# A GNN layer on one core: results handled in block order, n gate's half copied out of PSUM by ScalarE, start-up loads and planner costs rearranged

## The chip, the core and the metric

The kernel runs on 1 core of one Trainium2 chip. The metric is the device time of one execution, in microseconds (us). Three executions of the kernel before took 1700.17, 1704.7 and 1708.09 us, median 1704.7. Engines: PE is TensorE (matrix multiplication), DVE VectorE, ACT ScalarE, POOL GpSimd, SP SyncE, which only issues DMAs here.

## The reference, cut to what matters

64 graphs of 256 nodes with 256 features. All is float32.

```
h = maximum(layernorm(x), 0)                      # x: (64, 256, 256)
xc = transpose(h)
c = relu(bn1(conv1d(xc, conv1_w)))                # width 1
c = bn2(conv1d(c, conv2_w, pad 8))                # width 17, along the nodes
x_conv = transpose(relu(c + xc))
s = h @ w_se.T + b_se                             # 3 values a node
A = exp(-squared distance of s) * adj
x_nmp = A @ relu(h @ w_msg.T + b_msg)
gi = concat(x_conv, x_nmp) @ w_ih.T + b_ih        # 512 -> 768
gh = h @ w_hh.T + b_hh                            # 256 -> 768
r, z = sigmoid(gi_r + gh_r), sigmoid(gi_z + gh_z)
n = tanh(gi_n + r * gh_n)
out = x + (1 - z) * n + z * h
```

## The kernel before, in words

**Tiles and stages.** Graphs are worked in pairs (W = 512 columns: two graphs of 256 nodes, channels on partitions) and pairs in blocks of four (8 graphs); there are NP = 32 pairs and NB = 8 blocks. The 17-tap convolution is done by short Fourier-like transforms along the nodes: `forward` (DVE) makes the tiles U, V, PT and Sv of a block, PE multiplies them with 47 transformed filters (`begin`, `complete`, `product`, L930-L965), and `join` (DVE) transforms back. The filters are made once, in the start-up: `filter_steps` (L1278) multiplies the raw weights (`taps`) with `points`, ACT copies the results out of PSUM, and SP and POOL store them in turn in DRAM (`filt`). From there each block loads them again, one filter of 256 KB a time, into nine slots `wb` (`load_kinds`, L905).

**A block.** First come the products with the filters; between them stand pieces of other pairs' work (`message`, `embed`, `affinity`, `aggregate`). Then `gates(i)` to `gates(i+3)` compute the GRU gates of the four pairs. `gates` calls `seven` (L1155) twice, once for r and z, once for n; each takes two PSUM accumulators `acc0` and `acc1` (a ring of two, L573) and four `aux` banks (L572), and its matmuls run in the order of parts 1, 5, 2, 6, 7, 3, 4. Six of the nine slots hold sums of activations for these parts, one (`e`) a copy, two (`tz0`, `tz1`) tanh of z. Part 7 is the last reader of the sums `ah`, `axn`, `axc`; after `gates(i+3)` they are given back (L1475) and `load_kinds` (L1477) starts the filter loads of the next block. The boundary between blocks is thus: part 7, 3 and 4 of the last n gate, the rest of the next pair's `message`, then `begin(0)` of the next block, whose product needs a filter slot, Sv and a free accumulator.

**The n gate** (L1190-L1204). For each half `dc` of the channels ACT reads `gh_n` out of the accumulator's second half; DVE multiplies it with r; DVE then reads the first half of the accumulator (`halfs(p, 0)`, L1195) and adds. Until that last read the accumulator is not free. tanh (ACT), three DVE operations and two ACT copies into `back` follow; the copies take the 16-bit halves of the result apart.

**Results.** `finish` (L1245) transposes `back` by a DMA into `gn_tile`. `deliver` (L1260) puts the halves together again (two ACT copies), adds x to each graph by an accumulating DMA on POOL's queue (L1268), and writes each graph to DRAM by another (L1269). Both address DRAM through `rows` (L588): partition h*16 + b holds two node rows at b*16 + 2h, so the DRAM side is 8 x 16 runs of 2 KB. `blocks` (L609) has partition b*8 + h instead, and its DRAM side is 128 runs one behind the other.

**The order of the work** isn't the order of the calls. `Recorder.record` (L334) notes every operation with a cost by engine and shape, and `plan` (L388) then puts them into each engine's queue: PE's calls get due times from the running sum of PE's costs, all others a due time back from what needs them, and at each step the engine that can start first takes its most urgent call. DMA costs (L342-L351) and ACT costs (L362-L367) enter there. All instructions are emitted from one place and therefore have the line L371 in the profile; groups are told apart by the tiles' names. Calls between `nc.first = 0` (L704) and L721 keep their order ahead of all others.

**Start-up loads** (L704-L721), on SP's queue: x of four pairs, then for each half `dc` the first three groups of taps (112 partitions, `load_taps`) and the remaining 7 partitions of all 18 groups at once (`load_last_taps`), then points 1 to 3, then the further groups. A group's matmul needs both pieces. While the four pairs are normalized and go through the first convolution, `filter_steps((1, 2, 3, 3)[j])` (L1298) hands out nine of the 55 filter steps between them.

Of the kernel before, what the change touches and what calls it, by code (L numbers as in the profile page):

```python
# [14 lines left out]
U16 = mybir.dt.uint16  # L15
# [234 lines left out]
class Recorder:  # L250
# [83 lines left out]
    def record(self, engine, op, args, kw):  # L334
        method = getattr(getattr(self.nc, engine), op)
        out = kw["out"] if "out" in kw else args[0]
        ins = [v for v in list(args) + list(kw.values()) if isinstance(v, bass.AP) and v is not out]
        n = 1
        for s in out.shape[1:]:
            n *= s  # L340
        size = 0
        if op.startswith("dma"):  # L342
            if "transpose" in op:
                size, cost = 2.5, self.TURN
            elif "accum_op" in kw:
                size, cost = 2.3, 1.0
            else:
                k = max(self.share(out, ins[0]), 10 if engine == "gpsimd" else 1)
                run = min(self.run(v) for v in (out, ins[0]))
                size = n * out.shape[0] * WIDTH[out.dtype] * 16 / k / 330e3 * max(1, 1400 / run)  # L350
                cost = 0.35 if k > 10 and run > 1024 else 0.62  # L351
        elif engine == "tensor":
            cost = n / 597 + 0.006
            if op == "transpose":
                cost = out.shape[-1] / 1170
            elif args[1].shape[0] < 32:
                cost = 0.23
        elif engine == "vector":
            cost = {"bn_stats": 0.33, "bn_aggr": 0.07}.get(op, n / 960 + 0.07)
            if op == "tensor_mul" and n == 256:  # L360
                cost = 0.5
        elif engine == "scalar":  # L362
            cost = n / 1400 + (0.2 if op == "activation" else 0.12)
            if out.dtype == U16:
                cost = n / 860
            elif len(out.shape) == 3 and op == "activation" and n == 256:
                cost = 0.49  # L367
        else:
            cost = 1.1 if self.planned == 0 else 7.0 if ALU.pow in args else 2.0
        k = len(self.tasks)  # L370
        self.tasks.append(Task(engine, lambda: method(*args, **kw), cost, size, self.first))  # L371
        self.last[engine] = k
        if self.behind is not None:
            self.tasks[k].preds.add(self.behind)
        if self.first is not None:
            self.first += 1
        for v in ins:
            self.access(k, v, False)
        self.access(k, out, True)
        return k  # L380
# [106 lines left out]
def kernel(  # L487
# [124 lines left out]
    def load_x(i, eng=nc.sync):  # L612
        if i >= NP:
            return
        X[i] = SPARE[i].rearrange("p (q d) -> p q d", d=D) if i in SPARE else x_rows
        load_rows(X[i], x, i, eng, blocks if i <= PB else rows)
# [56 lines left out]

    def load_taps(dc, a, b, eng):
        v = c2_wT[dc * P + a * KG:dc * P + b * KG].rearrange("(g k) t o -> (k t) g o", k=KG)
        eng.dma_start(out=taps[:MAIN, a:b, dc, :], in_=v[:MAIN])

    def load_last_taps(dc, eng):
        v = c2_wT[dc * P:dc * P + FULL * KG].rearrange("(g k) t o -> (k t) g o", k=KG)
        eng.dma_start(out=taps[MAIN:KG * TAPS, :FULL, dc, :], in_=v[MAIN:])  # L680

    def load_last_group(dc, eng):
        last = c2_wT[dc * P + FULL * KG:(dc + 1) * P]
# [24 lines left out]
    load_points(0, nc.scalar)  # L708
    for j in range(PB):
        load_x(j)  # L710
    for dc in range(DC):
        load_taps(dc, *PARTS[0], nc.sync)
        load_last_taps(dc, nc.sync)
    for n in range(1, len(PASSES) + 1):
        load_points(n, nc.sync)
    for part in PARTS[1:]:
        for dc in range(DC):
            load_taps(dc, *part, nc.sync)
# [456 lines left out]
    def halfs(p, k):  # L1175
        return p[:, :, k * N:(k + 1) * N]

    def pieces(t):
        return t.rearrange("p (g n) -> p g n", n=N)

    def gates(i, between=None):
        tr, gn = tr_tile, gn_tile
        tz = [slots[ROLE[f"tz{dc}"]].rearrange("p c d -> p (c d)") for dc in range(DC)]

        def rz(dc, p):
            for gate, t in ((0, tr[:, dc]), (1, tz[dc])):
                nc.scalar.activation(pieces(t), halfs(p, gate), AF.Tanh,
                                     bias=b_rz[:, gate * DC + dc:gate * DC + dc + 1], scale=0.5 - dc)

        def n(dc, p):  # L1190
            g = gn[:, dc]
            nc.scalar.activation(pieces(g), halfs(p, 1), AF.Identity,
                                 bias=b_hh[:, 2 * DC + dc:2 * DC + dc + 1], scale=1.0 - 2 * dc)
            nc.vector.scalar_tensor_tensor(g, tr[:, dc], 1.0, g, op0=ALU.add, op1=ALU.mult)
            nc.vector.scalar_tensor_tensor(pieces(g), pieces(g), 0.5, halfs(p, 0), op0=ALU.mult,  # L1195
                                           op1=ALU.subtract if dc else ALU.add)
            nc.scalar.activation(g, g, AF.Tanh, bias=b_ih[:, 2 * DC + dc:2 * DC + dc + 1])
            d = tr[:, dc]
            nc.vector.tensor_sub(d, HT[i][:, dc], g)
            nc.vector.scalar_tensor_tensor(d, tz[dc], 1.0, d, op0=ALU.add, op1=ALU.mult)  # L1200
            nc.vector.scalar_tensor_tensor(d, d, 0.5, g, op0=ALU.mult, op1=ALU.add)
            u = d.bitcast(U16).rearrange("p (n j) -> p j n", j=2)
            for j in range(2):
                nc.scalar.copy(back.bitcast(U16).rearrange("p (c j n) -> p c j n", c=DC, j=2)[:, dc, j], u[:, j])  # L1204

        def last(dc, g, p):
            a = slice(g * N, (g + 1) * N)
            v, d = gn[:, dc, a], tr[:, dc, a]
            nc.scalar.activation(v, p[:, N:], AF.Identity,
                                 bias=b_hh[:, 2 * DC + dc:2 * DC + dc + 1], scale=1.0 - 2 * dc)  # L1210
            nc.vector.scalar_tensor_tensor(v, d, 1.0, v, op0=ALU.add, op1=ALU.mult)
            nc.vector.scalar_tensor_tensor(v, v, 0.5, p[:, :N], op0=ALU.mult, op1=ALU.subtract if dc else ALU.add)
            nc.scalar.activation(v, v, AF.Tanh, bias=b_ih[:, 2 * DC + dc:2 * DC + dc + 1])
            nc.vector.tensor_sub(d, HT[i][:, dc, a], v)
            nc.vector.scalar_tensor_tensor(d, tz[dc][:, a], 1.0, d, op0=ALU.add, op1=ALU.mult)
            for c in range(MC):
                t = chunk(y_last[:, dc], g, c).rearrange("p (b h) -> p h b", b=NW)
                u, w = (q[:, c * P:(c + 1) * P].rearrange("p (h b) -> p h b", b=NW) for q in (d, v))
                nc.vector.scalar_tensor_tensor(t, u, 0.5, w, op0=ALU.mult, op1=ALU.add)

        seven(i, RZ, rz)
        if between:
            between()
        if i + 1 < NP:
            seven(i, NH, n)
            return
        a0, p5, e1, a1, e0 = aux(), aux(), aux(), acc()[:, 1], acc()[:, 0]
        e = slots[ROLE["e"]].rearrange("p c d -> p (c d)")
        part(a0, 1, i, NH, True)
        nc.scalar.mul(e0, a0, -1.0)  # L1230
        part(p5, 5, i, NH, True)
        nc.scalar.copy(e, p5)
        part(a0, 2, i, NH)
        last(0, 0, a0)
        part(e0, 6, i, NH)
        nc.vector.tensor_add(a1, e0, e)
        part(e0, 7, i, NH)
        nc.vector.scalar_tensor_tensor(e1, e0, -1.0, e, op0=ALU.mult, op1=ALU.subtract)
        last(1, 1, e1)
        part(a1, 3, i, NH)  # L1240
        last(0, 1, a1)
        part(e0, 4, i, NH)
        last(1, 0, e0)
# [16 lines left out]
    def deliver(i):  # L1260
        y = back.rearrange("p (q d) -> p q d", d=D)
        t = gn_tile.rearrange("p c n -> p (c n)").bitcast(U16)
        v = y.bitcast(U16).rearrange("p q (c d j) -> p j c q d", c=DC, j=2)
        u = t.rearrange("p (c j q d) -> p j c q d", j=2, c=DC, d=P)
        for j in range(2):
            nc.scalar.copy(v[:, j], u[:, j])
        for g in range(G):
            nc.gpsimd.dma_start(out=row_tile(y, g), in_=rows(x, G * i + g), accum_op=ALU.add)  # L1268
            nc.gpsimd.dma_start(out=rows(out, G * i + g), in_=row_tile(y, g))  # L1269

    FIRST = PARTS[1][1]
    steps = deque((m, g) for g in range(FIRST) for m in range(len(PASSES)))
# [19 lines left out]
    for j in range(PB):  # L1292
        if j > 0:
            norm(j)
        transpose_h(j)
        conv1(j, True)
        split(j)
        filter_steps((1, 2, 3, 3)[j])  # L1298
    *bn2, b_ih, b_hh = columns("bn2")
    s2, h2_shift = fold_bn(bn2, "bn2", 1.0 / L)  # L1300
    b_rz = keep("b_rz", 2 * DC)
# [222 lines left out]
```

## Time and profile before

| | |
|---|---|
| three executions, us | 1700.17, 1704.7, 1708.09 |
| the profiled execution, us | 1703.87 |
| its span, first to last instruction, us | 1702.1 |
| TensorE clock granted, mean | 0.994 |
| DMA bytes moved | 261.47 MB, mean 154 GB/s |

| engine | busy, us | what runs on it |
|---|---|---|
| PE | 1666.3 | 8984 matmuls; a float32 matmul of the code is two of them |
| DVE | 1457.8 | transforms, gates, layernorm |
| ACT | 1052.4 | copies out of PSUM, exp, tanh, copies of 16-bit halves |
| POOL | 231.8 | 62 accumulating loads and 62 stores of results among its DMA issues |

An engine's busy time says how long its instructions ran; a group of instructions is shown with its count, busy time and mean, and with the idle time of the engine just ahead of it. The timeline has start, duration and, in brackets, the idle time ahead and what ended it. A block takes about 200 us: from 300 to 400 us lies mostly the products' part of one, from 400 to 500 us mostly the gates' part.

### The profile page before, as it was taken

What the parts mean: (1) busy time and instruction counts of PE and PEld (TensorE: products, weight loads), DVE (VectorE), ACT (ScalarE), POOL (GpSimd) and SP (SyncE); (2) the same over time, 40 slices, a digit from 0 to 9 for tenths busy, and PEclk for the clock granted to TensorE, in tenths of its full rate; (3) what the DMA queues carried; (4) which work ended last, traced back from release to release, by engine and by line L of the source; (5) the groups of instructions that cost most, each with busy time, mean ns of one, the idle gap of its engine ahead of it and who ended that gap; (6) DMA issues with size and microseconds to landing.
All of it is one profiled execution on the core that took longest, in us unless ns stands there. A gap on an engine that the chain in (4) does not pass through costs nothing.

```text
span 1702.1 us, 26181 instructions
## 1 busy us (share of the span) xinstructions
PE 1666.3 (98%) x8984; PEld 1420.8 (83%) x8984; DVE 1457.8 (86%) x3401; ACT 1052.4 (62%) x1967; POOL 231.8 (14%) x245
## 2 busy tenths in 40 slices
PE   8999999999999999999999999999999999999998
PEld 5888878988889788888888887897888978898886
DVE  7969989799889998799997998979987899879545
ACT  5546665685657765676655866567575766556453
POOL 4211130022110121102110021101211012100010
PEclk9999999999999999999999999999999999999999
DMA  9982666966579366773559554694756836484032
GB/s 228 306 280 69 137 117 142 280 136 140 108 196 241 94 127 124 218 208 89 122 113 293 136 116 110 160 273 97 144 112 191 233 91 125 88 245 129 17 60 52
DMA packets 326812, 261.47 MB, mean 154 GB/s; under 512 B 204751, under 2 KB 252139, under 8 KB 326678
## 3 DMA queue, kind: packets, MB, share of 16 engines
q1 hardware_dynamic: 296982, 216.71, 48.4%
q0 software_dynamic: 29280, 42.76, 13.1%
q8 instruction: 71, 1.16, 0.3%
q14 instruction: 63, 0.52, 0.1%
q10 hardware_dynamic: 416, 0.32, 0.1%
HBM read 156.60 MB, written 43.78 MB: 118 GB/s over the span
## 4 chain that ended last, share of the span: by engine, by line
PE 77%; DVE 17%; DMA 3%; issue 1%; ACT 1%; SPq 0%; DVEq 0%; ACTq 0%
PE acc L371 52%; PE aux L371 25%; DVE V L371 3%; DVE T L371 3%; DVE U L371 2%; DVE gn L371 2%; DMA wb<-filt 2%; DVE tr L371 1%; DVE acc L371 1%; DVE wb L371 1%; DVE Yv L371 1%; DVE PT L371 1%; DMA taps<-in_c_wT_dram 1%; DVE msg L371 1%; DMA filt<-Yv 0%
## 5 line engine op out<-in xcount | busy, mean ns | idle before, releaser
L371 PE MATMUL acc<-wb,w_ih 128*128 128x256 f32 x768 | 191.9, 379 | 0.0
L371 PEld LDWEIGHTS acc<-wb,w_ih 128*128 128x128 f32 x768 | 145.9, 190 | 19.8
L371 POOL DMA_DIRECT2D back<-in_x_dram x62 | 61.9, 1161 | 696.6 <-ACT back L371 622.5
L371 POOL TENSOR_TENSOR rstd<-rstd,neg_half 128x4 f32<-128x4 f32 x32 | 81.6, 2548 | 472.7 <-DVE shift L371 284.8
L371 PE MATMUL aux<-wb,w_x 128*128 128x256 f32 x576 | 141.6, 384 | 0.6 <-ACT e L371 0.5
L371 DVE SCALAR_TENSOR_TENSOR V<-T,V 128x128 f32<-128x128 f32 (+2 forms) x448 | 140.2, 377 | 0.0
L371 PE MATMUL acc<-wb,w_x 128*128 128x256 f32 x576 | 136.5, 381 | 1.8 <-DVE acc L371 1.5
L371 PEld LDWEIGHTS acc<-wb,w_x 128*128 128x128 f32 x576 | 107.9, 190 | 28.6 <-DVE acc L371 8.4
L371 PEld LDWEIGHTS aux<-wb,w_x 128*128 128x128 f32 x576 | 108.0, 191 | 20.2 <-issue 4.0
L371 PE MATMUL aux<-w_msg,hT 128*128 128x259 f32 x512 | 120.9, 381 | 0.0
L371 PE MATMUL acc<-V,wb 128*128 128x128 f32 x1024 | 119.0, 275 | 0.6 <-ACT acc L371 0.6
L371 PEld LDWEIGHTS acc<-U,wb 128*128 128x128 f32 x1024 | 117.4, 192 | 1.5 <-issue 0.5
L371 PE MATMUL acc<-U,wb 128*128 128x128 f32 x1024 | 118.2, 275 | 0.3 <-DMA wb<-filt 0.3
L371 PEld LDWEIGHTS acc<-V,wb 128*128 128x128 f32 x1024 | 116.7, 192 | 1.2 <-ACT acc L371 0.8
L371 PE MATMUL acc<-wb,w_hh 128*128 128x256 f32 x384 | 110.1, 381 | 0.7 <-ACT acc L371 0.7
L371 DVE TENSOR_TENSOR T<-Yv 128x512 f32<-128x512 f32 (+1 forms) x80 | 42.5, 580 | 79.4 <-ACT Yv L371 78.9
L371 PE MATMUL aux<-hT,w_c 128*128 128x512 f32 x224 | 107.3, 595 | 2.7 <-ACT e L371 2.7
L371 PE MATMUL acc<-Yv,w_ih 128*128 128x256 f32 x380 | 108.5, 381 | 0.1
L371 PEld LDWEIGHTS aux<-w_msg,hT 128*128 128x128 f32 x512 | 96.5, 190 | 14.3
L371 PE MATMUL acc<-hT,w_hh 128*128 128x256 f32 x380 | 104.7, 383 | 0.6 <-ACT acc L371 0.4
L371 PE MATMUL acc<-xnm,w_ih 128*128 128x256 f32 x380 | 103.9, 380 | 0.0
L371 ACT COPY back<-gn 128x1024 uint16<-128x1024 uint16 x62 | 80.5, 1348 | 36.6 <-DMA gn<-back 36.6
(194 smaller groups left out, 3842.1 us busy)
## 6 DMA issues: line engine op xcount, KB each, us to landing
wb<-filt SPq DMA_DIRECT2D x376, 256.0 KB
back<-in_x_dram POOLq DMA_DIRECT2D x62, 256.0 KB, 7.3
out_dram<-back POOLq DMA_DIRECT2D x62, 256.0 KB, 4.8
x<-in_x_dram SPq DMA_DIRECT2D x58, 256.0 KB
halves_d<-halves SPq DMA_DIRECT2D x28, 512.0 KB
adjh<-halves_d SPq DMA_DIRECT2D x112, 128.0 KB
hh<-halves SPq DMA_DIRECT2D x108, 128.0 KB
filt<-Yv POOLq DMA_DIRECT2D x18, 224.0 KB, 4.6
```

The costliest lines, as they stand in the source:

```text
L371: self.tasks.append(Task(engine, lambda: method(*args, **kw), cost, size, self.first))
```

## The change

Six edits.

1. `deliver` adds x and writes the result through `blocks` in place of `rows`. So that the partitions fit, the n gate's copies into `back` put the 512 columns in the order (graph half q, block b, place h) while they read (q, h, b); they become copies with four dimensions.
2. In the n gate ACT copies the first half of the accumulator into the pair's `XNM` tile (free by then), and DVE's second operation reads that in place of PSUM.
3. Taps are loaded with both pieces of a group range together: the 7 partitions of three, three and twelve groups, each behind its 112.
4. Points 1 and 2 are loaded ahead of the first taps, points 3 behind them.
5. `filter_steps` hands out (0, 2, 3, 4) steps with the four pairs in place of (1, 2, 3, 3).
6. Planner costs: an accumulating DMA counts 1.3 in place of 2.3 for its size; ACT's 16-bit copies count n/750 (1024 columns), n/840 (512 columns) or n/470 (four dimensions) in place of n/860. The queues of all engines are planned anew with these.

```diff
             elif "accum_op" in kw:
-                size, cost = 2.3, 1.0
+                size, cost = 1.3, 1.0
...
             if out.dtype == U16:
-                cost = n / 860
+                cost = n / 750 if n > 512 else n / 840 if len(out.shape) < 4 else n / 470
...
     def load_taps(dc, a, b, eng):
         v = c2_wT[dc * P + a * KG:dc * P + b * KG].rearrange("(g k) t o -> (k t) g o", k=KG)
-        eng.dma_start(out=taps[:MAIN, a:b, dc, :], in_=v[:MAIN])
-
-    def load_last_taps(dc, eng):
-        v = c2_wT[dc * P:dc * P + FULL * KG].rearrange("(g k) t o -> (k t) g o", k=KG)
-        eng.dma_start(out=taps[MAIN:KG * TAPS, :FULL, dc, :], in_=v[MAIN:])
+        for r in (slice(MAIN), slice(MAIN, KG * TAPS)):
+            eng.dma_start(out=taps[r, a:b, dc, :], in_=v[r])
...
+    for n in range(1, len(PASSES)):
+        load_points(n, nc.sync)
     for dc in range(DC):
         load_taps(dc, *PARTS[0], nc.sync)
-        load_last_taps(dc, nc.sync)
-    for n in range(1, len(PASSES) + 1):
-        load_points(n, nc.sync)
+    load_points(len(PASSES), nc.sync)
...
+            x = XNM[i][:, dc]
+            nc.scalar.copy(pieces(x), halfs(p, 0))
             nc.vector.scalar_tensor_tensor(g, tr[:, dc], 1.0, g, op0=ALU.add, op1=ALU.mult)
-            nc.vector.scalar_tensor_tensor(pieces(g), pieces(g), 0.5, halfs(p, 0), op0=ALU.mult,
-                                           op1=ALU.subtract if dc else ALU.add)
+            nc.vector.scalar_tensor_tensor(g, g, 0.5, x, op0=ALU.mult, op1=ALU.subtract if dc else ALU.add)
...
             u = d.bitcast(U16).rearrange("p (n j) -> p j n", j=2)
+            v = back.bitcast(U16).rearrange("p (c j n) -> p c j n", c=DC, j=2)[:, dc]
             for j in range(2):
-                nc.scalar.copy(back.bitcast(U16).rearrange("p (c j n) -> p c j n", c=DC, j=2)[:, dc, j], u[:, j])
+                nc.scalar.copy(v[:, j].rearrange("p (q b h) -> p q b h", h=L // 2, b=NW),
+                               u[:, j].rearrange("p (q h b) -> p q b h", h=L // 2, b=NW))
...
         for g in range(G):
-            nc.gpsimd.dma_start(out=row_tile(y, g), in_=rows(x, G * i + g), accum_op=ALU.add)
-            nc.gpsimd.dma_start(out=rows(out, G * i + g), in_=row_tile(y, g))
+            nc.gpsimd.dma_start(out=row_tile(y, g), in_=blocks(x, G * i + g), accum_op=ALU.add)
+            nc.gpsimd.dma_start(out=blocks(out, G * i + g), in_=row_tile(y, g))
...
-        filter_steps((1, 2, 3, 3)[j])
+        filter_steps((0, 2, 3, 4)[j])
```

## The prediction

> **What bounds the kernel now.** First the page's busy shares: PE is the bound, and nothing that shortens another engine counts unless PE waits for it.
>
> ```profile
> span 1702.1 us, 26181 instructions
> PE 1666.3 (98%) x8984; PEld 1420.8 (83%) x8984; DVE 1457.8 (86%) x3401; ACT 1052.4 (62%) x1967; POOL 231.8 (14%) x245
> ```
>
> The spacing of matmuls agrees: where nothing waits, 256 columns start every 0.215 us, 128 every 0.111, 512 every 0.429; spacing beyond that sums to 41 us over the span. So 41 us is all that there is to win. The change leaves PE's matmuls as they are, so I ask where these 41 us lie. In PE's timeline two kinds of place hold most.
>
> The first is the start:
>
> ```profile
> 15.10 1.04 PE L371 MATMUL aux<-ident,T 128*128 128x128 f32 x8
> 18.82 2.02 PE L371 MATMUL aux<-taps,points 119*112 119x256 f32 x4 [2.68 <-DMA taps<-in_c_wT_dram]
> 20.63 4.29 PE L371 MATMUL acc<-hT,w_c 128*128 128x512 f32 x8
> ```
>
> PE sat idle 2.68 us for a load of taps, with the second pair's convolution queued behind it.
>
> The second is the boundary between blocks. Six times PE idles there: 1.75, 2.28, 1.95, 2.40, 2.36 and 2.36 us (13.1 in all) before its first product of the next block; the seventh is 0.24. Timeline of PE, then the chain of work, of the third:
>
> ```profile
> 693.91 1.03 PE L371 MATMUL acc<-wb,w_ih 128*128 128x256 f32 x4
> 694.77 1.04 PE L371 MATMUL aux<-w_msg,hT 128*128 128x259 f32 x4
> 697.76 2.59 PE L371 MATMUL acc<-Sv,wb 128*128 128x128 f32 x11 [1.95 <-DMA wb<-filt]
> ```
> ```profile
> 691.94 5.68 DMA wb<-filt
> 697.62 0.14 issue
> 697.76 4.32 PE acc L371 x22
> ```
>
> The chain names a filter load that took 5.68 us. Other boundaries are put down to "DVE tr", which can't be: that operation touches neither slot nor accumulator. In the trace's semaphore updates all six starts lie 0.09 to 0.14 us behind the landing of the second filter load issued, the slot that the first product reads. Why is it late? POOL's timeline of the same window:
>
> ```profile
> 691.27 0.64 POOL L371 DMA_DIRECT2D out_dram<-back  x1 [4.52 <-DMA back<-in_x_dram]
> 693.00 0.63 POOL L371 DMA_DIRECT2D out_dram<-back  x1 [1.09 <-DMA back<-in_x_dram]
> ```
>
> A store of results is issued just ahead. The first filter load (issued 691.51) lands at 694.45, the second (691.94) only at 697.62, just behind the store (last update 696.98); the third at 698.27. At the seventh boundary, where both stores were over (1499.17), the same two loads took 2.73 and 2.94 us. So the store costs the second load 2.7 us. Its shape is odd: in the list of DMAs it takes longer than a load of equal size in block order on the same queue.
>
> ```profile
> back<-in_x_dram POOLq DMA_DIRECT2D x62, 256.0 KB, 7.3
> out_dram<-back POOLq DMA_DIRECT2D x62, 256.0 KB, 4.8
> adj<-in_adj_dram POOLq DMA_DIRECT2D x6, 256.0 KB, 3.5
> ```
>
> Undisturbed, the store's first update comes after 1.7 us and its last after 4.3; for the block-ordered adjacency they come after 2.5 and 2.75.
>
> [...] The new copies write 2-byte elements 16 bytes apart[...]; no run here shows such a copy.
>
> **The change part by part.**
>
> *Block order (1).* 124 DMAs change shape. Accumulating packets of 2 KB take 178 ns (median)[...]. Of two accumulates behind each other the first lands 1.4 us sooner (6.2 becomes 4.8 after issue), the second up to 2.8 (7.3 becomes 4.5 to 5.9). The stores follow that much earlier and last about 3 us (half of the 2.6 us spread off 4.3; bounds 2.75 and 4.3). At the third boundary: accumulates issued 684.78, stores issued about 689.9 and 690.6, done by 692.9 and 693.6. The second filter load (691.94) then lands near 694.9 to 695.5, and PE has other work until 695.81: the wait goes. What is late next? The accumulator: `acc0` is free when ACT has copied both halves. In the second boundary's timeline ACT's bias copy starts 492.69, lasts 0.69 and is followed by a copy of 0.58, so 493.9 against PE's 494.83. In the built order the first product writes `acc0` at all boundaries but the first, where it is `acc1`, free some 1.3 us later: about 0.4 us of wait. I leave 0.2 us a boundary: 13.1 - 1.2 = 11.9, say 12 us gained. Bounds: nothing (another reason stands behind the load), 13.3. If stores move only partly, each boundary keeps up to its 2 us. The rest of the deliveries lie beside matmuls that don't wait; nothing counted.
>
> *The price on ACT.* 124 copies into `back` rise from 617 ns. Bounds: the same 617, and twice that[...]. I take 1.09, what the diff itself writes for this shape (512/470). That is 124 x 0.47 = 58 us. ACT ends near 1147 us (67%) together with part 2.
>
> *PSUM half by ACT (2).* 62 new copies of 128 x 512 from PSUM, at the 575 ns of `acc<-acc`: 36 us on ACT. DVE's operation stays: 677 ns from PSUM, 678 for the like one from SBUF (`tr<-tr,gn`). Waits added: DVE's second operation now needs the copy, but its first (681 ns) runs beside it. Queued behind the copy on ACT are tanh of the first half and evictions for PE. `aggregate(i+2)` writes the same XNM buffer and must wait for DVE's read; in the built order it stands behind the tanh that needs that read anyway. Gained: the accumulator is free at about 0.6 us after ACT's bias copy, in place of two DVE operations; PE waits there today only at the boundaries and 0.14 us once at 227.9.
>
> ```profile
> L371 ACT COPY back<-tr 128x512 uint16<-128x512 uint16 x124 | 68.9, 617 | 18.4 <-DVE tr L371 18.4
> L371 ACT COPY acc<-acc 128x512 f32<-128x512 f32 x64 | 36.7, 575 | 49.4 <-PE acc L371 49.1
> 400.00:500.00 100.00, 97.26 (x451) 81.56 (x450) 94.35 (x238) 57.44 (x96) 17.67 (x16) 1.00 0.62 136
> ```
>
> The 94 us on ACT fall on 31 pairs, 12 us a block, mostly where ACT (fourth column) is busy 57 of 100 us: it becomes about 65. PE's cover is other matmuls; if that cover fails, a PE eviction waits for one copy, at most 1.1 us. Counted: +1.5 us over the whole, from 0 to +10.
>
> *Start (3 to 5).* At 18.82 PE waited for the second 7-partition piece ([...]landed 18.69); its 112-partition neighbour had landed at 15.99. With pieces of 21 KB (3 groups), less 216 KB and plus 109 KB of points ahead, the first group is there by about 15. The built order has both transposes of pair two first (done 15.7), one whole filter step (0.87 us), then the convolution, whose input ACT delivers at about 16.6 in place of 17.07. So it starts near 16.8, not 20.63; PE has then done 0.86 us of filter work in place of 1.29. Gain 3.83 - 0.43 = 3.4; part may be lost to the next wait (ACT's evictions), so I take the idle time itself, 2.7. Bounds 0 and 3.4. SP issues four DMAs more (12 pieces of taps in place of 8), about 0.45 us each, ahead of x of pair five (27.36) and the first filter store (29.0); the next user of that evicted buffer comes seven evictions later, past 40 us, so nothing is counted. The points' order has no further cost.
>
> *Planner (6).* Costs don't run on the chip; the queues change little. On PE, besides the start, single filter products and `message` matmuls trade places. On POOL the accumulates and stores keep their order; on SP several output transposes, x loads and adjacency loads move past a few others, filter loads keep their order but for some pairs. Counted zero, from -2 to +3.
>
> *Sum.* Profiled execution 1703.9 (span 1702.1 + 1.8): -12 - 2.7 + 1.5 = 1690.7. The median of the runs lies 0.8 above it: 1691.5, rounded 1691.
>
> **The rivals.** *A, the boundary keeps its wait:* the second load is late because two accumulates and nine loads share the memory[...]. For it: the same wait stands at 296.4, where the first store had ended at 291.95 and only the second was left. Against: at the seventh the loads are clean once stores are over. Time: 1704.7 - 2.7 + 1.5 = 1703.5. *B, slower:* [...]`seven` hands each unit over by an ACT copy between accumulators (part 6 waits for it). In the built order copies into `back` stand directly ahead of such hand-overs. Now these waits sum to under 10 us. If a hand-over is late by 1 us in each of 31 pairs, that is +31: 1704.7 - 14.7 + 31 = 1721. It decides from 0.75 us a pair (23 us, 8.5 net). Against: part 5 and part 2 lie between, 1.3 us each in the n gate. *C, the DMAs change but stores still overlap half:* 1704.7 - 6 - 2.7 + 1.5 = 1697.5.
>
> **How the numbers follow.** Forecast 55% (1685 to 1696), C 12% (1694 to 1700), A 19% (1700 to 1706), B 14% (above 1706). About 0.5%, 8.5 us, is what a measurement can tell from no change, so the line is 1696.2 and 1713.2. Faster: 52 of the forecast's 55 and 6 of C; slower: two thirds of B. The range reaches from 1685 to A's 1706; left out are 4 below and 14 above.
>
> **What would show it.** PE's idle time before the boundary product under 0.5 us at the six places; a store's landing near 3 us and an accumulate's near 5; no `taps` wait at 18.8; `back<-tr` near 1.1 us a copy and ACT at 1147 us; PE's busy time unchanged. Wrong would be a boundary wait of 2 us (A), or new `PE acc <- ACT` waits in the gates of more than 20 us (B).

## The result, and the profile after

The kernel before took 1707.3 us (median of five executions, 1700.17 to 1708.09), the changed kernel 1693.64 us (median of five, 1689.2 to 1694.44): a ratio of 0.9922, 95% interval 0.9897 to 0.9947, or 13 us less. The forecast was 1691 us, 13.7 us below the median of the three executions that the prediction had. The profiled execution took 1694.44 us.

The first lines of the page:

```profile
span 1692.7 us, 26271 instructions
PE 1662.7 (98%) x8984; PEld 1420.2 (84%) x8984; DVE 1458.6 (86%) x3401; ACT 1133.6 (67%) x2029; POOL 227.9 (13%) x245
```

PE is still the bound with the same matmuls. What fell is the time in which it waits: start-to-start spacing of matmuls beyond the undisturbed one sums to 9.7 us less than before, the span is 9.4 us shorter. ACT has 81 us more to do, and that doesn't show in the span.

The third boundary, PE's timeline and then POOL's:

```profile
694.87 1.03 PE L371 MATMUL acc<-wb,w_ih 128*128 128x256 f32 x4
695.73 0.60 PE L371 MATMUL aux<-w_msg,hT 128*128 128x259 f32 x2
696.63 3.81 PE L371 MATMUL acc<-Sv,wb 128*128 128x128 f32 x32 [0.30 <-ACT gn L371]
```
```profile
685.75 1.80 POOL L371 DMA_DIRECT2D back<-in_x_dram  x2 [26.24 <-ACT back L371]
690.07 0.58 POOL L371 DMA_DIRECT2D out_dram<-back  x1 [2.52 <-DMA back<-in_x_dram]
692.13 0.56 POOL L371 DMA_DIRECT2D out_dram<-back  x1 [1.48 <-DMA back<-in_x_dram]
```

A wait of 0.30 us stands where 1.95 stood. In the trace's semaphore updates the stores now give first and last signs of landing at 692.30 and 692.64, and at 694.78 and 695.46: spread over 0.3 to 0.7 us in place of 3.0 and 2.5. The filter loads behind them land one each 0.66 us (695.84, 696.50, 697.18), no longer with the hole of 3.2 us between first and second. The first product starts 0.13 us behind the second landing, so the same load still ends the wait, though the profile names ACT: only its lateness has gone. The list of DMAs and the costs on ACT:

```profile
back<-in_x_dram POOLq DMA_DIRECT2D x62, 256.0 KB, 5.4
out_dram<-back POOLq DMA_DIRECT2D x62, 256.0 KB, 2.8
```
```profile
L371 ACT COPY back<-tr 128x512 uint16<-128x512 uint16 x124 | 128.0, 1077 | 15.2 <-DVE tr L371 14.9
L371 DVE SCALAR_TENSOR_TENSOR gn<-gn,xnm 128x512 f32<-128x512 f32 x62 | 41.7, 679 | 0.3
L371 ACT COPY xnm<-acc 128x512 f32<-128x512 f32 x62 | 35.8, 577 | 0.0
```

The start looked as if it had gained nothing. The wait for taps is gone, but the second pair's convolution begins at 18.95, not near 16.8:

```profile
9.84 1.19 PE L371 MATMUL aux<-ident,x 128*128 128x128 f32 x8 [1.37 <-DVE x L371]
11.73 3.35 PE L371 MATMUL acc<-hT,w_c 128*128 128x512 f32 x4 [0.70 <-DVE hT L371]
18.09 1.03 PE L371 MATMUL aux<-taps,points 119*112 119x256 f32 x4
18.95 3.60 PE L371 MATMUL acc<-hT,w_c 128*128 128x512 f32 x8
```

and at about 116 us PE waits for filter loads that land at the same time as before. So I went into the experiments with two theories of the whole. The first, the prediction's own: block order alone brings about 12 us, since it frees the boundary's filter load, and the rest is small. The second: a good part comes from elsewhere, from the accumulator that the PSUM copy frees, or from the queues as the planner now orders them. For the start, theory G: its lead is given back.

### The profile page after: what moved, and what is told of

Its sections match the earlier page's. It is cut to its first block, busy times and chain, and to the rows that moved or that the text cites. A ratio compares the mean times of both kernels' runs of the same rounds, so it can differ in the third digit from the quotient of the medians.

```text
span 1692.7 us, 26271 instructions
## 1 busy us (share of the span) xinstructions
PE 1662.7 (98%) x8984; PEld 1420.2 (84%) x8984; DVE 1458.6 (86%) x3401; ACT 1133.6 (67%) x2029; POOL 227.9 (13%) x245
## 4 chain that ended last, share of the span: by engine, by line
PE 64%; DVE 29%; DMA 4%; issue 2%; ACT 2%; SPq 0%; DVEq 0%; ACTq 0%
PE acc L371 44%; PE aux L371 20%; DVE V L371 6%; DVE T L371 4%; DVE tr L371 4%; DVE U L371 3%; DVE wb L371 3%; DMA wb<-filt 3%; DVE gn L371 2%; DVE acc L371 2%; DVE Yv L371 1%; DVE PT L371 1%; DVE st L371 1%; DVE msg L371 1%; DMA hh<-halves 1%
## 5 line engine op out<-in xcount | busy, mean ns | idle before, releaser
L371 POOL DMA_DIRECT2D back<-in_x_dram x62 | 56.8, 1056 | 750.8 <-ACT back L371 717.5
L371 ACT COPY back<-tr 128x512 uint16<-128x512 uint16 x124 | 128.0, 1077 | 15.2 <-DVE tr L371 14.9
L371 ACT ACTIVATE gn<-acc,bn_columns 128x512 f32<-128x512 f32 (+1 forms) x64 | 43.5, 680 | 97.2 <-PE acc L371 85.6
L371 PE MATMUL aux<-e,msg 128*128 128x256 f32 x448 | 103.6, 380 | 0.0
```

## The experiments

The ratio is that to the kernel before, run on the same chip in the same set; microseconds are the ratio's share of 1706 us. The rows come from three chips, so rows of different sets are compared by their ratios. "Boundary waits" are PE's lost time just ahead of the first product at the seven boundaries, from the spacing of matmuls in the profiled execution; "waits for e" are the row of PE's waits for the exp copies `e` that ACT makes out of PSUM. Both come from one execution of each kernel.

| edits made | label | ratio, 95% interval | us | boundary waits, us | waits for e, us |
|---|---|---|---|---|---|
| none | before | 1 | 0 | 14.5 | 3.2 |
| 1 | e1_blocks | 0.9997, 0.9986 to 1.0007 | -0.5 | 3.4 | 7.3 |
| 1, its DMAs only | e7_plain_copies | 0.9963, 0.9949 to 0.9977 | -6.3 | 3.4 | 4.5 |
| 2 | e3_copyout | 1.0042, 1.0030 to 1.0054 | +7.2 | 12.7 | 3.6 |
| 3 to 5 | e2_start | 0.9977, 0.9968 to 0.9985 | -3.9 | 14.3 | |
| 6 | e4_costs | 1.0044, 1.0023 to 1.0064 | +7.5 | 10.0 | 5.0 |
| 1, 2 | f2_blocks_copyout | 1.0000, 0.9986 to 1.0014 | 0 | 0.0 | 11.9 |
| 1, 6 | f1_blocks_costs | 0.9977, 0.9967 to 0.9988 | -3.9 | 6.7 | 2.3 |
| 2, 6 | f3_copyout_costs | 0.9989, 0.9979 to 1.0000 | -1.9 | 12.6 | 4.5 |
| 1, 2, 6 | e5_no_start | 0.9941, 0.9927 to 0.9954 | -10.1 | 4.4 | 2.3 |
| 1, 3 to 6 | e6_no_copyout | 0.9966, 0.9955 to 0.9977 | -5.8 | 6.6 | 2.3 |
| all | after_again | 0.9926, 0.9911 to 0.9942 | -12.6 | 1.5 | 2.3 |

The edits don't add. 1, 2 and 6 by themselves sum to +14 us; together they are at -10.

**Block order alone.** Edit 1 on the kernel before:

```diff
+                nc.scalar.copy(v[:, j].rearrange("p (q b h) -> p q b h", h=L // 2, b=NW),
+                               u[:, j].rearrange("p (q h b) -> p q b h", h=L // 2, b=NW))
...
+            nc.gpsimd.dma_start(out=row_tile(y, g), in_=blocks(x, G * i + g), accum_op=ALU.add)
+            nc.gpsimd.dma_start(out=blocks(out, G * i + g), in_=row_tile(y, g))
```

> The kernel before with edit 1 alone (results handled in block order, copies into back permuted); PSUM copy, start and planner costs as before. Theory S[...]: the six boundary waits of 13.1 us leave less than 0.5 us each, the store lands near 3 us after issue, and the whole comes out 9 to 12 us below the kernel before. Rival P (part of the gain comes from the accumulator that the PSUM copy frees sooner): the boundary keeps waits of 0.5 to 1.3 us on the accumulator, gain only 4 to 7 us. Rival R (the gain is one of the re-planned queues, not of the DMAs): boundary waits stay near 2 us, gain under 3 us.

Measured: no change. The boundary waits went from 14.5 to 3.4 us (six of the seven are 0.40 us, one is 1.00), nearly as theory S (the stores by rows held the second filter load up) said, and yet the time stayed: the gain came back as other waits. The largest part, 4.1 us, is in the gates, in PE's waits for `e`; 2.1 us are in its waits for ACT's `acc` and 1.9 us in those for DVE's `msg`. ACT's timeline of this kernel, then PE's:

```profile
842.97 4.00 ACT L371 COPY back<-tr 128x512 uint16<-128x512 uint16 x4
846.84 1.23 ACT L371 ACTIVATE e<-aux 128x256 f32<-128x256 f32 x4
```
```profile
845.59 0.71 PE L371 MATMUL aux<-zT 9*128 9x256 f32 x8
847.31 1.12 PE L371 MATMUL aux<-hT,w_c 128*128 128x512 f32 x2 [1.01 <-ACT e L371]
848.27 1.03 PE L371 MATMUL acc<-wb,w_x 128*128 128x256 f32 x4
```

PE writes the distances into an `aux` bank at 845.59; ACT should copy them out through exp, but four permuted copies are queued ahead, 4.00 us where four of the old ones would be 2.5 (4 x 617 ns). The next matmuls want the bank, and wait 1.01 us. That comes in every block from the third on, where the kernel before waits 0.45. Why do four stand there? With 860 elements a microsecond the planner holds a copy for 0.6 us; it takes 1.07.

**Its DMAs without its copies.**

```diff
-            nc.gpsimd.dma_start(out=rows(out, G * i + g), in_=row_tile(y, g))
+            nc.gpsimd.dma_start(out=blocks(out, G * i + g), in_=row_tile(y, g))
```

(and the accumulate likewise; the copies into `back` as before, so this kernel leaves out the reordering and gives the nodes in another order than the reference's)

> Block order in the two DMAs of a delivery only; the copies into back stay contiguous, so the results land in DRAM, and x is added, in another order of nodes than the reference's. Planner costs, PSUM half and start as before. It takes the price of the permuted copies away and keeps what the DMAs give. Theory K and theory S of the first set: copies at 617 ns, as the planner counts them, no gate waits, no boundary waits: 8 to 12 us less than before. Rival (the gates' waits come from the re-planned queues or from DMAs that now collide elsewhere, not from long copies): within 3 us of before.

Measured: 6.3 us less, with boundary waits as in edit 1 and copies of 616 ns. So the DMAs are worth 6 us, and the permuted copies cost about 6 us (e7 against e1) where the planner doesn't know their length: it counts 0.6 us for them in both kernels, so the order of all queues is the same and only the copies' length differs. Less than the 8 to 12 us expected, more than the rival's 3: the boundary gave 11.1 us, and waits for `e` rose from 3.2 to 4.5 us, those for DVE's `msg` from 0.2 to 2.7, so the re-planned queues took part of it back.

**Block order with the costs, and with the PSUM copy.**

```diff
-                cost = n / 860
+                cost = n / 750 if n > 512 else n / 840 if len(out.shape) < 4 else n / 470
```

(on top of edit 1, with the accumulate's 1.3)

> The kernel before with edits 1 and 6 (block order and planner costs; start and PSUM half as before). Theory K (block order alone gained nothing because the planner counts the permuted copies at 0.6 us where they take 1.07, and so queues four of them ahead of exp copies that TensorE waits for; edit 6 cures that): the gates' waits of 0.6 to 1.2 us go, the boundary waits stay gone, 6 to 10 us less than before. Rival V (it is the PSUM copy that gives the gates their slack): within 2 us of block order alone, that is of the kernel before.

```diff
+            x = XNM[i][:, dc]
+            nc.scalar.copy(pieces(x), halfs(p, 0))
...
+            nc.vector.scalar_tensor_tensor(g, g, 0.5, x, op0=ALU.mult, op1=ALU.subtract if dc else ALU.add)
```

(on top of edit 1, costs as before)

> The kernel before with edits 1 and 2 (block order and PSUM copy; start and planner costs as before). Theory K: the copies are still planned at 0.6 us, so the gates keep their waits: within 3 us of the kernel before, or slower as edit 2 alone was. Rival V: 6 to 10 us less than before.

Measured: 3.9 us less and no change; neither the 6 to 10 us that theory K had for the costs nor those that rival V had for the copy. Each does its own part. With the costs the waits for `e` fall from 7.3 to 2.3 us; four permuted copies in a row occur 2 times in the profile, 10 times without. The copy alone takes the boundary waits to nothing, but leaves the copies in fours, and the waits for `e` grow to 11.9 us (1.52 us a block from 443 us on). The changed kernel has both; ACT's timeline at the same place as above:

```profile
837.74 3.01 ACT L371 COPY back<-tr 128x512 uint16<-128x512 uint16 x3
840.64 0.66 ACT L371 ACTIVATE e<-aux 128x256 f32<-128x256 f32 x2
841.18 1.07 ACT L371 COPY back<-tr 128x512 uint16<-128x512 uint16 x1
842.13 0.68 ACT L371 ACTIVATE e<-aux 128x256 f32<-128x256 f32 x2
```

The fourth copy has moved between two pairs of exp, and PE doesn't wait for `e` there. It does wait at that place for something else:

```profile
840.95 2.86 PE L371 MATMUL acc<-wb,w_x 128*128 128x256 f32 x12 [0.43 <-DVE acc L371]
```

This is a hand-over in `seven`, where PE waits for DVE's sum `acc`. Over the whole of the changed kernel that row has grown; before, then after:

```profile
PE acc L371 <- DVE acc L371: 1.5, 3, 0.7
PE acc L371 <- DVE acc L371: 5.3, 11, 1.1
```

It is 4.4 us in f1 and in e6 and 5.5 in e5, but 2.0 in e1 and 1.5 in f2: on block order it comes with edit 6, and is what the new order costs, near 4 us that the change leaves behind.

**The changed kernel without its PSUM copy.**

```diff
-            nc.scalar.copy(pieces(x), halfs(p, 0))
...
+            nc.vector.scalar_tensor_tensor(pieces(g), pieces(g), 0.5, halfs(p, 0), op0=ALU.mult,
+                                           op1=ALU.subtract if dc else ALU.add)
```

> The changed kernel with edit 2 undone (VectorE reads the n gate's half from PSUM again). Prediction's step: 0.6 us less than the changed kernel, since 36 us of ScalarE go. Theory K: the same as the changed kernel within 2 us, 8 to 12 us less than before. Rival V: most of the gain goes, within 4 us of before.

Measured: 5.8 us less than before, so 6.8 us of the gain hang on edit 2. That is nearer to rival V than to theory K, though neither number was met. Two rows of waits hold about as much: at the boundaries 6.6 us in place of 1.5 to 2.3, and for DVE's `msg` 4.0 in place of 0.9. The third boundary, PE's timeline and the chain of work:

```profile
689.01 0.60 PE L371 MATMUL aux<-w_msg,hT 128*128 128x259 f32 x2
690.53 3.81 PE L371 MATMUL acc<-Sv,wb 128*128 128x128 f32 x32 [0.92 <-DVE gn L371]
```
```profile
688.91 0.59 DVE gn L371
689.51 0.06 DVE st L371
689.57 0.20 issue
689.77 0.67 DVE gn L371
690.44 0.09 issue
690.53 3.47 PE acc L371 x29
```

The second filter load had landed at 689.22 and PE was free at 689.61. What PE waits for is DVE's second operation of the n gate, which reads the accumulator until 690.44, one DVE operation of statistics in between. Was this wait there before, hidden behind the later filter load? Only a small part of it. In the kernel before the same read ends at 695.96, about 0.15 us after PE's matmuls (695.81). With the filter load in time and the costs as before (e1, third boundary, PE and then DVE) it shows as 0.24 us:

```profile
699.46 1.04 PE L371 MATMUL aux<-w_msg,hT 128*128 128x259 f32 x4
700.74 1.46 PE L371 MATMUL acc<-Sv,wb 128*128 128x128 f32 x11 [0.24 <-issue]
```
```profile
699.96 0.68 DVE L371 SCALAR_TENSOR_TENSOR gn<-gn,acc 128x512 f32<-128x512 f32 x1
```

It is 0.24 or 0.25 us at six of seven boundaries of e1 and of e7. In f1 and e6, which have edit 6, it is 0.92 at three and at four of them. Two things differ there: PE has two matmuls of `message` left in place of four (0.60 us in place of 1.04), and statistics stand around DVE's first operation. So edit 2 mostly takes away a wait that edit 6 brings. It is not the only one: f1 at its third boundary waits 1.09 us for its filter load, which ran beside a store.

**The PSUM copy without block order,** with and without the costs. First edit 2 alone (its diff is above):

> The kernel before with edit 2 alone (ScalarE copies the n gate's first half out of PSUM, VectorE reads the copy). Prediction: beside other work, 0 to +0.6 us, bounds 0 to +4. Rival P (accumulator free sooner): 1 to 4 us less than before, with shorter waits of TensorE for accumulators; since the boundary waits for a filter load either way, I expect none of that here. Rival B (ScalarE's hand-overs delayed): 4 us more or above, in TensorE waits for ScalarE.

Then with edit 6:

> The kernel before with edits 2 and 6 (PSUM copy and planner costs), results by rows as before. Theory Q (the boundary has two waits behind each other, first the filter load, then the accumulator; the PSUM copy removes the second only): the boundary keeps about 2 us a block, and the whole is within 3 us of the kernel before. Rival V (the PSUM copy with right costs is what brings the 6 us that it brings on top of block order): 5 to 8 us less than before.

Measured: 7.2 us more, and 1.9 us less. Theory Q holds: both keep the boundary waits (12.7 and 12.6 us of 14.5). The chain of work at the third boundary of f3:

```profile
691.68 5.88 DMA wb<-filt
697.55 0.14 issue
697.69 2.47 PE acc L371 x10
```

An accumulator that is free sooner is of no use while the filter is late. For the +7.2 us I expected 0 to 0.6. The number is rival B's, its mechanism is not seen: PE's waits for ACT's `e` and `acc` are 3.6 and 1.6 us (3.2 and 1.7 before). Those for DVE's `acc` rose from 1.5 to 3.6, and no single wait accounts for the whole: up to 118 us PE lost 1.8 us more than before, ahead of the matmuls of `acc<-wb,w_x` and `aux<-wb,w_x` 4.7 us more. Why the planner's order with 62 short copies more does that stays open.

**The costs alone.** Edit 6 on the kernel before; the value for four dimensions applies to nothing there.

> The kernel before with edit 6 alone (planner costs: accumulates 1.3 in place of 2.3, ScalarE's 16-bit copies n/840 and n/750 in place of n/860; the value for four dimensions applies to nothing here). Prediction: 0, from -2 to +3. Theory K (the costs matter through the permuted copies): within 3 us of before. Rival (better queues bring a gain of their own, whatever the shape of the copies): 4 us less or better.

Measured: 7.5 us more, outside all that was expected. Prices nearer to the measured ones, for copies that didn't change, made the order worse: PE's waits for DVE's `msg` are 3.7 us where the kernel before has 0.2, and those for `e` 5.0 against 3.2. How the planner comes to that order from those prices I didn't settle.

**The start alone, and the change without it.**

```diff
+        for r in (slice(MAIN), slice(MAIN, KG * TAPS)):
+            eng.dma_start(out=taps[r, a:b, dc, :], in_=v[r])
...
-        filter_steps((1, 2, 3, 3)[j])
+        filter_steps((0, 2, 3, 4)[j])
```

> The kernel before with edits 3 to 5 alone (taps with both pieces together, points ahead, filter steps 0, 2, 3, 4). The prediction's step: 2.7 us less. Theory G (the lead is given back): TensorE reaches the products with V about 2.4 us sooner (near 101 us from the start of the span, 103.3 before) but then waits for a filter load at about 116 us, as in the kernel before, since the stretch from 60 to 116 us is bound by the DMAs; the whole is within 1 us of the kernel before.

> The changed kernel with edits 3 to 5 undone (start as in the kernel before; block order, PSUM copy and planner costs kept). The prediction's steps: 10.5 us less than before, so 2.7 us more than the changed kernel. Theory G (the start's lead is given back at about 116 us): the same as the changed kernel within 1 us, that is 9 to 10 us less than before or better.

Measured: 3.9 us less by itself; without it the change still brings 10.1 us (10.5 were expected). Theory G falls for the start alone: the lead is kept. Beside the other edits it is worth 2.5 us by the two ratios, 0.9926 and 0.9941, whose intervals overlap, so there its size is not settled.

**The changed kernel once more.**

> The changed kernel, unaltered, beside the kernel before and the three others of this set, so that the runs without the start edits and without the PSUM copy have a reference with more executions, and the start a second profile. If the start edits are worth what was predicted (2.7 us), the second pair's convolution starts near 17 us from the start of the span, as in the run without the PSUM copy (16.92), and the first profile (18.95) was an execution with a late start; the whole is 11 to 14 us less than before. If the start's lead is given back (theory G), it is no faster than the run without the start edits, 10 us less than before.

Measured: 0.9926, as at first. PE's timeline of its start:

```profile
11.10 1.98 PE L371 MATMUL acc<-hT,w_c 128*128 128x512 f32 x4 [0.71 <-DVE hT L371]
15.86 1.03 PE L371 MATMUL aux<-taps,points 119*112 119x256 f32 x4
16.73 3.60 PE L371 MATMUL acc<-hT,w_c 128*128 128x512 f32 x8
```

The convolution begins at 16.73, as in e2 (16.71) and e6 (16.92); the first profile, at 18.95, had caught an execution whose first convolution began 0.63 us later and ran at a granted clock of 0.57 on the mean (3.35 us in place of 1.98). My reading that the start gained nothing was a reading of one execution.

**An attempt at more.** From 105 to 116 us the mean busy share of the 16 DMA engines is 0.99 in the changed kernel's profile, and the weights `w_ih` and `w_hh` (2.36 MB) are loaded in it.

```diff
+            nc.behind = nc.last["scalar"]
             nc.gpsimd.dma_start(out=w_hh, in_=hh_wT.rearrange("(k p) o -> p k o", p=P))
             nc.gpsimd.dma_start(out=w_ih, in_=ih_wT.rearrange("(k p) o -> p k o", p=P))
+            nc.behind = None
```

> The changed kernel with one edit more: the loads of the GRU weights w_ih and w_hh (2.36 MB, issued near 102 us, first used near 126 us) wait for ScalarE's copies of the first products, so that they no longer share the DMA engines with the filter loads between 102 and 116 us. Theory D (that stretch is bound by the DMAs, and TensorE's waits of 1 to 2 us near 116 us come from it): the waits go, 1 to 4 us less than the changed kernel. Rival (filter loads are held by their own number or by their late issue): within 1 us of the changed kernel. If weight sums come too late for the first gates: slower by 1 to 3 us.

Measured: 0.9919 (0.9905 to 0.9934), the same as the changed kernel. It tests nothing: the two loads are still issued at 100.38 and 101.16 us, 101.71 and 102.50 in the changed kernel, presumably because the ACT operation that `nc.behind` names was over by then. Whether theory D is right stays open. It serves as a further profile of nearly the same queues: span 1686.9 us.

## Why the prediction was right, and where only its sum was

*Block order, -12 us.* The mechanism is right as far as the traces show it: the store by rows held the second filter load up, and it moved half as many packets at a time. From 150 to 1560 us the packets of 4 KB on POOL's queue, nearly all of them the stores', are under way for 137.0 us in the kernel before, most often 8 at a time (42% of that time); in the changed kernel for 72.1 us, most often 16 at a time (19%). The accumulates' packets of 2 KB go the same way, most often 8 (26%), then 16 (18%), at a median of 178 ns each in both kernels. An accumulate has 128 of them: by these numbers I estimate 2.85 us with 8 at a time and 1.42 with 16, and the difference is the 1.4 us that the prediction gives the first accumulate. The semaphore updates of the kernel before agree: of the load's sixteen signs of landing at the third boundary eight come at 694.58 to 695.35 and eight only at 696.70 to 697.62, and the store's own come in two eights as well (693.95 to 694.67, 696.05 to 696.98). In the changed kernel the same load's sixteen come at 695.90 to 696.50. On which DMA engine a packet ran, and how the store kept the load's other eight back, the traces don't show. In the changed kernel all six waits are shorter, five of them under 0.5 us and the fourth 0.99 us (one of 1.25 us has come up among the first products of the fifth); the store lands at 2.8 us (about 3 was forecast) and the accumulate at 5.4 (4.8 for the first, up to 5.9 for the second). Rivals A and C are out. The size at the boundary is right too: the DMAs alone (e7) took 11.1 us of waits from it, and the accumulator then held PE 0.24 us a boundary, where 0.2 was left for it (worked out with edit 2; e7 has none). But the time fell by 6.3 only, and with the permuted copies (e1) by nothing. The step that failed is "The rest of the deliveries lie beside matmuls that don't wait; nothing counted": the same edit re-plans the queues, and the waits came back elsewhere, for `e`, for `msg` and, with long copies, for more of `e`.

*ACT's price, +1.5 us.* 1077 ns a copy against 1.09 forecast, ACT 1133.6 us against 1147. These copies took 1.75 times the 617 ns of the old ones. The prediction had their pattern the wrong way round, though: as the diff writes them they put their 2-byte elements down side by side and read them 64 bytes apart (16 places of 4 bytes), where the old ones read them 4 bytes apart. What in this pattern costs the time was not shown; that there would be a price was an estimate. The price in time was taken as +1.5 (0 to +10): with the costs known to the planner it is about 2 (f1 against e7; the intervals overlap, so that isn't settled), without them 6. So rival B's mechanism was real: long copies ahead of a hand-over. It acts at another place than I put it, the exp of `affinity`, at some 1 to 1.5 us a block, and edit 6 is what keeps it off. The hand-overs in `seven` got later with edit 6 too, by 4 us in all, but where the chain of work was followed (439.97 us) it runs through DVE's transforms, not through ACT's copies.

*PSUM half by ACT, 0.* DVE's time is as forecast (679 ns), the copy 577. It was booked as no gain of its own, and by itself it is none (+7.2); e6 gives 6.8 us for it in its place. There it removes the wait for the accumulator that edit 6's order made longer.

*Start, -2.7 us.* By itself 3.9 (2.6 to 5.5), in the company of the others perhaps 2.5; the convolution starts at 16.7 to 16.9 where 16.8 was worked out.

*Planner, 0 (-2 to +3).* This step failed: "Costs don't run on the chip; the queues change little". The costs don't run on the chip, but the order that they make does. Alone they are +7.5 us, on edit 1 -3.4 (f1 against e1), on edit 2 -9.1 (f3 against e3), on edits 1 and 2 -10.1 (e5 against f2). With that order edits 1 and 2 pay. That truer prices make better queues is not shown by this: the same values made them worse in e4, and on edit 2 they gained where no copy is permuted.

The sum, -13.2, met the measured -12.6 and -13.3 because 12 us were booked for "the boundary wait goes, nothing else comes". Edits 1, 2 and 6 together come near that (-10.1, where the parts add up to -10.5), and none of them alone does. That the new order turned out well is luck as far as the prediction goes: it was booked at 0, and was worth anything from -10.1 to +7.5 us with what stood beside it.

## What to carry to other kernels

Where one wait ends at a place, list what would end it next, in the queues as each edit leaves them: the same accumulator was 0.24 us late in one order and 0.92 in another. A wait that is gone counts only when the time has gone too; 11 us fewer at the boundaries were 6 us, and with long copies none. When an operation's cost changes under a planner that uses costs, the planner's number is part of the edit; measure with and without it. Take a difference of 2 us near the start of one profiled execution for nothing until a second profile shows it.

## What the runs showed of the hardware

A stall of PE cost more than its length in some of these profiles. Busy time, with the granted clock behind PE's to POOL's columns, around the third boundary of the kernel before, whose stall ends at 697.76:

```profile
693.00:696.00 3.00, 2.81 (x13) 2.11 (x12) 3.00 (x11) 1.39 (x3) 0.62 (x1) 1.00 0.95 247
696.00:697.76 1.76, 0.00 (x1) 0.03 (x1) 1.76 (x4) 1.47 (x6) 0.00 (x0) 1.00 0.90 269
697.76:701.00 3.24, 3.24 (x16) 3.24 (x16) 3.24 (x8) 1.00 (x2) 0.00 (x0) 0.51 0.92 338
701.00:704.00 3.00, 3.00 (x27) 3.00 (x27) 1.81 (x9) 1.28 (x3) 1.67 (x2) 0.96 0.84 270
```

After 1.95 us of idle time the clock is at 0.51 for 3.2 us: 16 products run in place of some 29 (3.24 us at the 0.111 us of an undisturbed one), and by the clock I estimate 1.6 us more lost (0.49 of 3.24). Over the 14 profiles of this case, leaving out a stall of 1.84 us at the start of each that no dip followed, 18 of 41 stalls of 1.5 to 2.9 us were followed by a mean clock under 0.9 in the next 3 us, and 4 of 57 stalls of 0.8 to 1.5 us. What decides whether a dip follows was not shown. The changed kernel's profile has no stall of 1.5 us or more between 150 and 1550 us; the kernel before lost clock at two of its six (0.50 in the 3 us behind each). Dips with no stall ahead of them occur as well (138.5 to 145.3 us in the changed kernel, at 0.50, PE busy throughout).

The mean clock also orders executions of one kernel: over the 251 executions of the experiments a mean clock lower by 0.001 went with 1.3 us more (correlation -0.75 within a kernel). The kernel before had 0.992 in the last set and the changed one 0.994, so by my estimate from these numbers some 2 of its 12.6 us come as clock, which fits fewer long stalls but was not tested by itself.
